# Ending the routed blocks two units sooner, and placing the first steps of the last layer beside the last two gated units

## The chip, the cores and the metric

The kernel runs on one core of a Trainium2 chip. The metric is the device time of one execution in microseconds; the time given for a kernel is the median of its runs. The core's engines work side by side, each through its own queue in order: TensorE (PE in the profile, its weight loads PEld), VectorE (DVE), ScalarE (ACT) and GpSimd (POOL); SyncE (SP) issues most DMAs, GpSimd issues the indirect ones. TensorE's results go to PSUM, eight banks, and are taken from there by VectorE or ScalarE.

## What is computed

Four layers, each of the form x = x + attention(norm(x)) + ffn(norm(x)), on 4 sequences of 512 tokens with 256 features in float32. What matters here is the end of layer 2 and the start of layer 3:

```
xn = layernorm(x)                                   # layer 2
x  = x + gated_attention(xn)                        # 16 heads, gated linear attention
       + latent_attention_and_experts(xn)           # 7 routed experts, top 2, and a shared one
xn = layernorm(x)                                   # layer 3
x  = x + xn + causal_attention(layernorm(xn)*g + b) # one head of 256 features
       + routed_moe(xn)                             # 8 experts of width 512, top 2, softmax of the two logits
```

## The kernel before

**Tiling.** x lies in on-chip memory as 16 tiles of 128 tokens, 4 to a sequence (b = 0 to 3). `xn` is its norm, `xnT` the transposed norm.

**Layer 2** (`layer2`, line 992) runs 32 gated units, one for each pair of heads and each sequence; unit u belongs to sequence u mod 4. A unit is split into three generators: `gated_supply` (line 1129: keys, queries, their exponentials, prepared one unit ahead), `gated_unit` (line 1174: scores, sums, softmax, products, gate, root of squares) and `gated_drain` (line 1314: transposes and output products of the unit before, which add into x). `run(u, beside, rate)` steps them in an order written as a string, line 1032: "m" is the unit, "s" the next one's supply, "d" the last one's drain. After each letter it takes `rate` steps, on average, of a further generator `beside`. For units 0 to 23 that is the latent attention; for units 24 to 30 it is `routed2` (line 1065): the dispatch of the tokens to 38 blocks of 128 slots, then for each block a fetch of weights and rows, a transposition, the hidden products and the output, which a GpSimd indirect DMA sends to a table in memory (`send_back`, line 330). Ahead of unit 31 the rest of `routed2` is run, and `collect` (line 338) reads the table back, two tiles of 256 KB for each two tiles of x, and adds them into x on VectorE. The order that the engines see is set by a scheduler from the order of the program and from its own model of durations; only in layer 3 is TensorE's order that of the program (line 1681).

**Layer 3** (`layer3`, line 1655) loads its weights, then for each sequence takes the norm (`layer_norm3`, line 1758: sums on VectorE, powers on GpSimd, and a second norm's scale `again`), the transposed features and the router (`route3`, line 1772: eight logits a token, the best two, softmax). Beside sequences 1 and 2 it starts the causal attention of sequences 0 and 1. `causal` (line 1789) is a generator whose first step adds xn into x on GpSimd, scales y on ScalarE, transposes it to yT and makes four qk products; the further steps are v, four steps of scores, the last transposition, the product with v, and the output. When all four routers are done, `dispatch` (line 158) counts the tokens of each expert (the rank and count matmuls), gives each a slot, and builds the table of slots with 64 small matmuls, eight `slots_on` steps; these are called beside the attention of sequences 0 and 1 from step 8 of their remaining steps on. Then 39 blocks run through the stages fetch, features, hidden, a pause and output, with the attention of sequences 2 and 3 beside them; `collect` and the stores of x end the kernel.

**Memory.** The latent attention's constants (rk, up, ow, rotk, rotq, va, and the tile mt of maxima) are tiles of a pool from layer 0 to the end of layer 2 (`latent_ahead`, line 1344). `Ring` is a helper that cuts tiles out of a given piece of memory by tag. In layer 2 four PSUM banks belong to the gated units (tag "ps") and, from unit 24 on, four to the routed blocks (tag "ex").

## Time and profile before

| | |
|---|---|
| median of 3 runs | 2320.91 us (2320.03 to 2325.61) |
| the profiled execution | 2334.37 us, of which the span from first to last instruction is 2332.6 us |
| mean granted TensorE clock | 0.909 |
| PE busy | 2019.1 us (87%) |
| DVE busy | 1240.0 us (53%) |
| ACT busy | 841.1 us (36%) |
| POOL busy | 625.8 us (27%) |
| the chain that ended last | PE 64%, DVE 12%, issue 10%, DMA 6%, POOL 5%, ACT 3% |

Times in the profile are microseconds from the start of the span. A line such as "L1216 PE MATMUL pt<-Wg,xnT 128x256 x8" is a run of eight matmuls issued at line 1216 that write tile pt from Wg and xnT; a float32 matmul of the program is two instructions. The granted clock is the share of TensorE's full speed that was allowed in the stretch. The profile cuts the span also into stages given by their ends, and then shows for each the busy time of every engine; busy time of TensorE times the clock is the work done, as it would be counted at full clock.

### The profile page before, as it was taken

To read this page: it belongs to the slowest core of one execution; us is meant where nothing else is said; L and a number is where in the kernel's file an instruction comes from. 1 tells how busy PE (TensorE), PEld (TensorE's weight loads), DVE (VectorE), ACT (ScalarE), POOL (GpSimd) and SP (SyncE) were. 2 spreads that over 40 slices of the span, in tenths; PEclk is the share of its full clock that TensorE was granted. 3 is DMA by queue.
4 is the path that set the end of the run, shared out by engine and by line. 5 is a ranking of instruction groups with operands and counts; after the bars stand their busy time and mean duration, and the time that the engine had idled before them with its cause. 6 is when DMAs were issued, how large, how long until landed. Compare 5 with 4: busy or idle time off the path is not lost.

```text
span 2332.6 us, 36307 instructions
## 1 busy us (share of the span) xinstructions
PE 2019.1 (87%) x13455; PEld 1501.4 (64%) x13455; DVE 1240.0 (53%) x3682; ACT 841.1 (36%) x1729; POOL 625.8 (27%) x737
## 2 busy tenths in 40 slices
PE   6754088874999999999999999999999968899995
PEld 2453077762566676666766676656778755678995
DVE  5765056657655655565565656546555564422223
ACT  1110056552334443343344444332354413344221
POOL 5334634443111121111111121110444332012331
PEclk8855599996999999999999999998999977899998
DMA  9911378874000000000000000001433220166897
GB/s 314 331 42 58 108 271 280 281 255 146 1 8 10 6 12 6 5 17 6 4 14 5 8 10 5 8 10 39 133 113 110 86 79 19 61 224 237 291 330 242
DMA packets 152536, 244.02 MB, mean 105 GB/s; under 512 B 15846, under 2 KB 111944, under 8 KB 152232
## 3 DMA queue, kind: packets, MB, share of 16 engines
q1 hardware_dynamic: 137336, 199.50, 26.3%
q0 software_dynamic: 15024, 42.20, 5.2%
q8 instruction: 107, 1.75, 0.3%
q14 instruction: 69, 0.57, 0.1%
HBM read 190.41 MB, written 66.58 MB: 110 GB/s over the span
## 4 chain that ended last, share of the span: by engine, by line
PE 64%; DVE 12%; issue 10%; DMA 6%; POOL 5%; ACT 3%; SPq 1%; another core or an unknown queue 0%; POOLq 0%; DVEq 0%; ACTq 0%
PE pt L1216 7%; PE pj L1138 6%; PE g L1742 5%; PE o L1329 4%; PE kq L1551 3%; PE sc L1201 3%; PE pov L1280 2%; PE gu L959 2%; PE o L1755 2%; DMA r<-l_rows,in_slot 2%; PE qk L1519 2%; DVE junk L1526 2%; PE pv L1567 2%; DMA r<-l_rows 2%; PE qkp L1804 1%
## 5 line engine op out<-in xcount | busy, mean ns | idle before, releaser
L334 POOL DMA_INDIRECT l_outs<-y,to x172 | 168.5, 980 | 325.5 <-ACT y L333 243.2
L306 DVE TENSOR_TENSOR mine<-r,number 128x2 f32<-128x2 f32 (+1 forms) x96 | 15.5, 161 | 273.9 <-DMA r<-l_rows,in_slot 207.2
L294 POOL DMA_INDIRECT r<-l_rows,in_slot x77 | 77.1, 1001 | 276.9 <-PE rt L325 147.0
L1742 PEld LDWEIGHTS g<-rT,we 128*128 128x128 f32 x1248 | 145.2, 192 | 5.2 <-ACT rT L327 3.4
L1742 PE MATMUL g<-rT,we 128*128 128x128 f32 x1248 | 145.9, 275 | 2.4 <-ACT rT L327 2.4
L1526 DVE CUSTOM_DVE_ANT_0 junk<-qk,hide 128x512 f32<-128x512 f32 (+3 forms) x256 | 124.7, 487 | 43.5 <-PE qk L1519 24.9
L1559 POOL TENSOR_SCALAR_AFFINE_SELECT pr<-pr 128x512 f32<-128x512 f32 x64 | 40.2, 639 | 339.3 <-ACT pr L1556 339.3
L959 PE MATMUL gu<-rT,we 128*128 128x128 f32 x760 | 112.5, 287 | 21.4 <-issue 9.7
L325 PE MATMUL rt<-ident,r 128*128 128x128 f32 x344 | 67.1, 295 | 70.2 <-DMA r<-l_rows 69.0
L327 ACT COPY rT<-rt 128x256 f32<-128x256 f32 x172 | 62.6, 372 | 178.3 <-PE rt L325 103.1
L1329 PE MATMUL o<-Wo,oT 128*128 128x256 f32 x512 | 126.2, 390 | 0.0
L959 PEld LDWEIGHTS gu<-rT,we 128*128 128x128 f32 x760 | 104.3, 198 | 33.7 <-issue 16.3
L1216 PE MATMUL pt<-Wg,xnT 128*128 128x256 f32 x512 | 124.2, 394 | 1.3 <-PE ot L1322 0.5
L333 ACT ACTIVATE y<-o,share 128x256 f32<-128x256 f32 x172 | 81.2, 473 | 114.9 <-PE o L1755 48.1
L1207 DVE TENSOR_TENSOR s<-sc,keep 128x512 f32<-128x512 f32 x128 | 82.5, 684 | 72.4 <-PE sc L1201 72.3
L1216 PE MATMUL pt<-Wv,xnT 128*128 128x256 f32 x512 | 120.1, 385 | 0.0
L1151 DVE RECIPROCAL rz<-rz 128x128 f32<-128x128 f32 x128 | 117.5, 935 | 0.4
L1216 PEld LDWEIGHTS pt<-Wg,xnT 128*128 128x128 f32 x512 | 97.0, 195 | 26.0 <-issue 7.1
L413 PE MATMUL tr<-ident,xn 128*128 128x128 f32 x160 | 33.7, 357 | 85.8 <-DVE xn L398 81.3
L1216 PEld LDWEIGHTS pt<-Wv,xnT 128*128 128x128 f32 x512 | 95.0, 191 | 15.1 <-DVE st L387 0.2
L1556 ACT ACTIVATE pr<-kq 128x512 f32<-128x512 f32 (+1 forms) x192 | 86.2, 530 | 50.1 <-PE kq L1551 49.5
L325 PEld LDWEIGHTS rt<-ident,r 128*128 128x128 f32 x344 | 53.9, 203 | 77.6 <-issue 75.0
(457 smaller groups left out, 4565.1 us busy)
## 6 DMA issues: line engine op xcount, KB each, us to landing
we<-l_packed SPq DMA_DIRECT2D x133, 384.0 KB
we<-l_w SPq DMA_DIRECT2D x78, 512.0 KB
we<-l_wo SPq DMA_DIRECT2D x39, 512.0 KB
l_rows<-none SPq DMA_DIRECT2D x1, 12920.0 KB
r<-l_rows SPq DMA_DIRECT2D x19, 680.0 KB
xn<-l_outs SPq DMA_DIRECT2D x32, 256.0 KB
l_rows<-xn SPq DMA_DIRECT2D x8, 544.0 KB
l_packed<-l_w_gate SPq DMA_DIRECT2D x1, 4096.0 KB
```

Of the source, the lines that this page charges most:

```text
L325: nc.tensor.transpose(pt[:, k, :], r[:, :D].rearrange("p (d k) -> p k d", k=KD)[:, k, :], self.ident)
L333: nc.scalar.activation(y, ps, AF.Copy, scale=share)
L334: self.no_order(moe["name"] + " back", nc.gpsimd.indirect_dma_start(out=moe["outs"][:, :], out_offset=bass.IndirectOffsetOnAxis(ap=to, axi ...
L959: nc.tensor.matmul(ps[:, q, :], we[:, q, k * P : (k + 1) * P], rT[:, k, :], start=(k == 0), stop=(k == KD - 1))
L1138: nc.tensor.matmul(ps, w[n][:, k, :], self.xnT[:, k, t["b"] * T : (t["b"] + 1) * T], start=(k == 0), stop=(k == KD - 1))
L1151: inverse = lambda c: nc.vector.reciprocal(rz[:, c * P : (c + 1) * P], rz[:, c * P : (c + 1) * P])
L1207: nc.vector.tensor_tensor(s, ps[hh], keep4, ALU.mult)
L1216: nc.tensor.matmul(ps[:, i, :], self.xnT[:, k, s : s + P], w[n][:, k, :], start=(k == 0), stop=(k == KD - 1))
L1329: nc.tensor.matmul(ps[:, p, :], of_parity(oT[:, h, c * D : (c + 1) * D], p), wo[:, h, :], start=(h == 0), stop=(h == 1),)
L1526: nc.vector.tensor_tensor_reduce(out=junk[:, :m], in0=tiles[j][:, off : off + m], in1=self.hide[:, T - m :], op0=ALU.add, op1=ALU.max, sca ...
L1556: nc.scalar.activation(pr[:, j, off : off + m], tiles[j][:, :m], AF.Exp, scale=0.25)
L1742: nc.tensor.matmul(pt[:, m, :], we[:, q, k * T + m * P : k * T + (m + 1) * P], rT[:, k, :], start=(k == 0), stop=(k == KD - 1),)
```

## The change

The routed blocks are stepped at 1.45 a letter instead of 1.25 and end with unit 29. `collect` takes a range of tiles, and for layer 2 it adds the two parts of a token on GpSimd first, so that VectorE adds once. It runs step by step beside unit 30, at 0.75 a letter, with the norm and router of sequence 0 (`ended2`). Beside unit 31, at 1.0 a letter, run norms and routers of sequences 1 and 2 (`ahead3`). The last unit's letters leave the supply out and have its drains sooner. Beside the last drain lie the first three steps of the causal attention of sequence 0. Layer 3's router state, loads and first tiles need memory at that time: they lie in two pieces, `both` and `mt`, that are shared with the latent attention's constants (`router3`); and their PSUM tiles come from the "ex" banks through an alias in `Ring`. `route3` and the first part of `causal` have more yields, and the add of xn into x comes after the qk products. Layer 3 then begins with the norm of sequence 3, v of sequence 0 and the products of sequence 1; the slots begin at step 4 of the remaining attention steps.

```diff
@@ -58,7 +58,11 @@
 
         self.base, self.free = base, 0
 
+    alias = None
+
     def tile(self, shape, dtype, tag, name, bufs=None):
+        if self.alias:
+            return self.pool.tile(shape, dtype, tag=self.alias, name=name)
         if tag not in self.places and self.pool is None:
             n = 1
             for d in shape[1:]:
@@ -89,6 +93,9 @@
         nc.gpsimd.memset(self.rows[:, :, D:], 0.0)
         self.xn = self.rows[:, :, :D]
         self.xnT = state.tile([P, KD, NB * T], F32, tag="xnT", name="xnT")
+
+        self.mt = state.tile([P, 4, P], F32, tag="mt", name="mt")
+        self.both = state.tile([P, 6144], F32, tag="both", name="both")
...
@@ -335,9 +342,9 @@
             out=moe["outs"][:, :], out_offset=bass.IndirectOffsetOnAxis(ap=to, axis=0), in_=y, in_offset=None
         ))
 
-    def collect(self, moe, wk):
-
-        for i in range(0, NTILE, 2):
+    def collect(self, moe, wk, of=range(0, NTILE, 2)):
+
+        for i in of:
             x = self.x[:, i : i + 2, :]
             ys = []
             for m in range(moe["k"]):
@@ -345,7 +352,7 @@
                 s = (m * NTILE + i) * P
                 self.load(y, moe["outs"][s : s + 2 * P, :].rearrange("(n p) d -> p n d", p=P))
                 ys.append(y)
-            if len(ys) > 2:
+            if len(ys) > 2 or moe is self.moe2:
                 self.nc.gpsimd.tensor_tensor(ys[0], ys[0], ys.pop(), ALU.add)
             for y in ys[1:] + ys[:1]:
                 self.nc.vector.tensor_tensor(x, x, y, ALU.add)
@@ -1029,7 +1036,7 @@
                 drain = self.gated_drain(units[u - 1]) if u else iter(())
                 credit = 0.0
                 chains = {"m": self.gated_unit(units[u]), "s": supply, "d": drain}
-                for what in "mmmmsmsmmdmmsmsdmsd":
+                for what in "mmmmsmsmmdmmsmsdmsd" if u + 1 < UNITS else "mmmmdmmdmmdmmm":
                     next(chains[what], None)
                     credit += rate
                     while credit >= 1:
@@ -1051,16 +1058,40 @@
                     pass
             wk = tp("ex", 4)
             gp["ex"] = tp("exps", 4, space=PSUM)
+            self.router3()
             routed = self.routed2(wk)
-            for u in range(first, UNITS):
-                if u == UNITS - 1:
-                    for _ in routed:
-                        pass
-                    self.collect(moe, wk)
-                run(u, routed, 1.25)
-            for _ in self.gated_drain(units[UNITS - 1]):
+            for u in range(first, UNITS - 2):
+                run(u, routed, 1.45)
+            for _ in routed:
                 pass
+            run(UNITS - 2, self.ended2(wk, gp["ex"]), 0.75)
+            run(UNITS - 1, self.ahead3(gp["ex"]), 1.0)
+            drain = self.gated_drain(units[UNITS - 1])
+            for chain in (self.units3[0], self.units3[0], drain, self.units3[0], drain, drain):
+                next(chain, None)
         self.held.close()
+
+    def ended2(self, wk, pool):
+
+        for i in range(0, NTILE, 2):
+            self.collect(self.moe2, wk, (i,))
+            yield
+            if i == 2:
+                self.layer_norm3(0)
+        yield from self.route3(0, pool, "ex")
+
+    def ahead3(self, pool):
+
+        self.layer_norm3(1)
+        for _ in range(3):
+            yield
+        yield from self.route3(1, pool, "ex")
+        for _ in range(5):
+            yield
+        self.layer_norm3(2)
+        for _ in range(2):
+            yield
+        yield from self.route3(2, pool, "ex")
 
     def routed2(self, wk):
 
@@ -1345,9 +1376,12 @@
 
         nc, a, NR = self.nc, self.a, 7
         tile = lambda n, *shape: wp.tile(list(shape), F32, tag=n, name=n)
-        kvq, rk, up = tile("kvq", P, KD, P), tile("rk", P, KD, T), tile("up", P, 2, T)
-        vu, ow, ln1, shift_row = tile("vu", 64, D), tile("ow", P, KD, D), tile("ln1", P, D), tile("shift_row", P, 1)
-        rotk, rotq = tile("rotk", P, T), tile("rotq", P, 2, T)
+        both = Ring(self.both, None)
+        cut = lambda n, k, m: both.tile([P, k, m], F32, tag=n, name=n, bufs=1)
+        kvq, rk, up = tile("kvq", P, KD, P), cut("rk", KD, T), cut("up", 2, T)
+        vu, ow, ln1, shift_row = tile("vu", 64, D), cut("ow", KD, D), tile("ln1", P, D), tile("shift_row", P, 1)
+        rotk, rotq = cut("rotk", 1, T)[:, 0, :], cut("rotq", 2, T)
+        va = cut("va", 4, 512).rearrange("p a (b c) -> p a b c", c=32)
         rw, rb, ln2, sh = tile("rw", P, KD, NR), tile("rb", 1, NR), tile("ln2", P, D), tile("sh", P, 3, D)
         kp = lambda ap: ap.rearrange("(k p) n -> p k n", p=P)
         self.load(kvq, kp(a["l2_kvq"]))
@@ -1370,7 +1404,7 @@
             self.load(sh[:, q].rearrange("p (k i) -> p k i", k=KD), kp(a["l2_sh_" + n]))
         self.load(sh[:, 2], a["l2_sh_down"])
         self.w2, self.top2 = tile("w2", P, NTILE, 8), tile("top2", P, NTILE, 8)
-        mt, va, sign = tile("mt", P, 4, P), tile("va", P, 4, 16, 32), tile("sign", P, 1)
+        mt, sign = self.mt, tile("sign", P, 1)
...
@@ -1654,50 +1688,39 @@
 
     def layer3(self):
         nc, a = self.nc, self.a
-        NE = 8
         with ExitStack() as ctx:
             tp = lambda n, bufs, **k: ctx.enter_context(self.tc.tile_pool(name=n, bufs=bufs, **k))
             self.wexp = tp("wexp3", 4)
             wp = tp("l3w", 1)
-            w = wp.tile([P, NTILE, NE], F32, tag="w", name="w")
-            top = wp.tile([P, NTILE, NE], F32, tag="top", name="top")
             moe = self.moe3
-            gw = wp.tile([P, KD, NE], F32, tag="gw", name="gw")
-            self.load(gw, a["l3_gate_w"].rearrange("(k p) n -> p k n", p=P))
-            wa, wk, we = tp("l3a", 1), tp("l3k", 2), tp("l3e", 4)
-            self.ps3 = ps3 = {n: tp("l3" + n, bufs, space=PSUM) for n, bufs in (("tr", 2), ("mm", 4), ("sm", 2))}
-            self.again = {}
-            ptr, psm = ps3["tr"], ps3["sm"]
...
+            self.wk3, we = tp("l3k", 2), tp("l3e", 4)
+            self.ps3 = ps3 = {n: tp("l3" + n, bufs, space=PSUM) for n, bufs in (("tr", 2), ("sm", 2), ("mm", 4))}
+            psm = ps3["sm"]
 
 
             with self.tc.manual_schedule(engines={mybir.EngineType.PE}):
-                units = [self.causal(b, gb, qkv, ow, wk, ps3) for b in range(NB)]
-                for b in range(NB):
+                units = self.units3
+                route = self.route3(NB - 1, psm, "sm")
+                with self.tc.high_priority():
+                    self.layer_norm3(NB - 1)
+                next(units[0])
+                for _ in range(2):
                     with self.tc.high_priority():
-                        self.layer_norm3(b)
-                        self.to_features(ptr, self.xn[:, 4 * b : 4 * b + 4, :], self.xnT[:, :, b * T : (b + 1) * T])
-                        self.route3(b, gw, wk, psm, w, top)
-                    if b in (1, 2):
-                        next(units[b - 1], None)
+                        next(route)
+                    next(units[1])
+                next(units[1])
                 pieces = self.wexp.tile([P, 3, 4, D], F32, tag="we", name="pieces")
                 pieces = Ring(pieces.rearrange("p q e d -> p (q e d)"), None)
-                slots = self.dispatch(moe, self.rows, top, w, pieces, psm, "sm", wp)
+                slots = self.dispatch(moe, self.rows, self.top3, self.w3, pieces, psm, "sm", wp)
 
                 def slots_on():
                     with self.tc.high_priority():
                         return next(slots, slots) is None
 
                 slots_on()
+                next(units[1])
                 for n, _ in enumerate(step for pair in zip(units[0], units[1]) for step in pair):
-                    if n >= 8:
+                    if n >= 4:
                         slots_on()
                 while slots_on():
                     pass
@@ -1755,6 +1778,30 @@
             self.nc.tensor.matmul(o, h[:, m, :], we[:, 2, m * D : (m + 1) * D], start=(m == 0), stop=(m == 3))
         self.send_back(self.moe3, o, to, share, wk)
 
+    def router3(self):
+
+        mt = self.mt.rearrange("p a b -> p (a b)")
+        cut = lambda at, a, b: mt[:, at : at + a * b].rearrange("p (a b) -> p a b", b=b)
+        self.w3, self.top3, self.gw3 = cut(0, NTILE, 8), cut(P, NTILE, 8), cut(2 * P, KD, 8)
+        self.cut3 = Ring(mt[:, 2 * P + 16 :], None, {"lg": (2, 4, 14), "ex": (2, 4, 8)})
+        self.gb3 = cut(2 * P + 16 + 112 + 64, 2, KD)
+        self.load(self.gw3, self.a["l3_gate_w"].rearrange("(k p) n -> p k n", p=P))
+        self.again = {}
+        both = Ring(self.both, None)
+        cut = lambda n, k, m: both.tile([P, k, m], F32, tag=n, name=n, bufs=1)
+        self.qkv3, self.ow3 = cut("qkv", KD, 3 * D), cut("ow", KD, D)
+        self.load(self.qkv3, self.a["l3_qkv"].rearrange("(k p) n -> p k n", p=P))
+        self.load(self.ow3, self.a["l3_o_proj"].rearrange("(k p) n -> p k n", p=P))
+        gb = self.gb3
+        for m in range(2):
+            for k in range(KD):
+                self.load(gb[:, m, k : k + 1], self.a["l3_gb"][m, k * P : (k + 1) * P].unsqueeze(1))
+        self.both3 = {n: cut(n, k, m) for n, k, m in (("y", 4, D), ("yT", KD, T), ("qk", 4, T))}
+        ex = Ring(None, self.gp["ex"])
+        self.ps3 = {n: ex for n in ("tr", "mm", "sm")}
+        ex.alias = "ex"
+        self.units3 = [self.causal(b) for b in range(NB)]
+
     def layer_norm3(self, b):
 
         nc = self.nc
@@ -1769,41 +1816,49 @@
         self.rsqrt(c, v, 1.0, 1e-5)
         self.again[b] = c
 
-    def route3(self, b, gw, wk, psm, w, marks):
-        nc = self.nc
-        ps = psm.tile([P, 4, 8], F32, tag="sm", name="lg")
+    def route3(self, b, pool, tag):
+
+        nc, gw, wk = self.nc, self.gw3, self.cut3
+        self.to_features(pool, self.xn[:, 4 * b : 4 * b + 4, :], self.xnT[:, :, b * T : (b + 1) * T], tag)
+        yield
+        ps = pool.tile([P, 4, 8], F32, tag=tag, name="lg")
         for i in range(4):
             for k in range(KD):
                 nc.tensor.matmul(ps[:, i, :], self.tokens(k, 4 * b + i), gw[:, k, :], start=(k == 0), stop=(k == KD - 1))
-        lg = wk.tile([P, 4, 14], F32, tag="lg", name="lg")
+        lg = wk.tile([P, 4, 14], F32, tag="lg", name="lg", bufs=2)
         nc.gpsimd.memset(lg, NEG)
         nc.vector.tensor_copy(lg[:, :, :8], ps)
         top, v8 = self.top_weights(lg, 8, 2)
-        nc.vector.tensor_copy(marks[:, 4 * b : 4 * b + 4, :], top)
-        ex = wk.tile([P, 4, 8], F32, tag="ex", name="ex")
+        nc.vector.tensor_copy(self.top3[:, 4 * b : 4 * b + 4, :], top)
+        ex = wk.tile([P, 4, 8], F32, tag="ex", name="ex", bufs=2)
         nc.vector.tensor_tensor(ex, lg[:, :, :8], v8[:, :, 0:1].to_broadcast([P, 4, 8]), ALU.subtract)
         nc.scalar.activation(ex, ex, AF.Exp)
         nc.vector.tensor_tensor(ex, ex, top, ALU.mult)
-        self.share(w[:, 4 * b : 4 * b + 4, :], ex)
-
-    def causal(self, b, gb, qkv, ow, wk, ps3):
-
-        nc = self.nc
-        ptr, pmm = ps3["tr"], ps3["mm"]
+        self.share(self.w3[:, 4 * b : 4 * b + 4, :], ex)
+        yield
+
+    def causal(self, b):
+
+
+        nc, qkv, ow = self.nc, self.qkv3, self.ow3
         x, xn = (t[:, 4 * b : 4 * b + 4, :] for t in (self.x, self.xn))
-        nc.gpsimd.tensor_tensor(x, x, xn, ALU.add)
-        y = wk.tile([P, 4, D], F32, tag="y", name="y")
+        place = lambda n, k, m: self.wk3.tile([P, k, m], F32, tag=n, name=n, bufs=1) if b % 2 else self.both3[n]
+        y = place("y", 4, D)
         for i in range(4):
             nc.scalar.activation(y[:, i, :], xn[:, i, :], AF.Copy, scale=self.again[b][:, i : i + 1])
-        yT = wk.tile([P, KD, T], F32, tag="yT", name="yT")
-        self.to_features(ptr, y, yT, gb=gb)
-        qk = wk.tile([P, 4, T], F32, tag="qk", name="qk")
+        yT = place("yT", KD, T)
+        self.to_features(self.ps3["tr"], y, yT, gb=self.gb3)
+        yield
+        qk = place("qk", 4, T)
         for m in range(4):
-            ps = pmm.tile([P, T], F32, tag="mm", name="qkp")
+            ps = self.ps3["mm"].tile([P, T], F32, tag="mm", name="qkp")
             for k in range(KD):
                 nc.tensor.matmul(ps, qkv[:, k, m * P : (m + 1) * P], yT[:, k, :], start=(k == 0), stop=(k == KD - 1))
             nc.scalar.copy(qk[:, m, :], ps)
-        yield
+            if m % 2:
+                yield
+        ptr, pmm, wk = self.ps3["tr"], self.ps3["mm"], self.wk3
+        nc.gpsimd.tensor_tensor(x, x, xn, ALU.add)
         v = wk.tile([P, 4, D], F32, tag="v", name="v")
         for j in range(0, 4, 2):
             ps = pmm.tile([P, 2, D], F32, tag="mm", name="vp")
```

## The prediction

> **What bounds the kernel now.** I read four views: the page's busy slices, the engines by stage, the timelines of TensorE, VectorE and GpSimd round the change of layers, and the groups of instructions in single windows. By stage (start:end, length, then busy microseconds and instruction counts of PE, PEld, DVE, ACT, POOL, then granted clock, DMA share, GB/s):
>
> ```profile
> 1836.00:1875.50 39.50, 37.01 (x266) 29.30 (x262) 19.87 (x53) 16.47 (x35) 13.50 (x15) 1.00 0.20 62
> 1875.50:1933.20 57.70, 34.05 (x201) 27.21 (x200) 34.30 (x76) 8.98 (x15) 26.41 (x32) 0.76 0.24 75
> 1933.20:1975.90 42.70, 34.98 (x145) 23.54 (x145) 16.68 (x101) 18.99 (x45) 6.23 (x15) 0.79 0.09 26
> 1975.90:2055.10 79.20, 70.43 (x266) 48.59 (x266) 33.61 (x176) 25.97 (x65) 3.42 (x4) 0.85 0.32 112
> 2055.10:2306.80 251.70, 249.95 (x1784) 232.50 (x1784) 66.09 (x303) 82.80 (x168) 71.87 (x74) 1.00 0.77 260
> ```
>
> The stages are gated unit 30; unit 31 with its drain; norms, features and routers of layer 3; dispatch and attention of sequences 0 and 1; expert blocks. Units and blocks are TensorE at full clock. The three stages between are not: busy time times clock is 25.9, 27.6 and 59.9, so 113.4 us of full-clock work takes 179.6 us, and 66.2 us are lost. The timelines show how (start, length, instruction, in brackets the idle time before it and what ended it; PE, then DVE, then POOL):
>
> ```profile
> 1909.89 1.12 PE L1269 MATMUL pvt<-ident,pv 128*128 128x128 f32 x4 [13.98 <-ACT pv L1256]
> 1913.80 3.61 PE L1329 MATMUL o<-Wo,oT 128*128 128x256 f32 x8
> 1919.99 2.00 PE L1329 MATMUL o<-Wo,oT 128*128 128x256 f32 x8
> 1926.42 0.66 PE L1322 MATMUL ot<-ident,o 128*128 128x128 f32 x4 [4.43 <-POOL o L1309]
> ...
> 1898.56 2.08 DVE L351 TENSOR_TENSOR x<-x,sum 128x512 f32<-128x512 f32 x1
> 1900.66 0.65 DVE L351 TENSOR_TENSOR x<-x,sum 128x512 f32<-128x512 f32 x1
> 1906.35 2.23 DVE L351 TENSOR_TENSOR x<-x,sum 128x512 f32<-128x512 f32 x1
> ...
> 1897.21 2.89 POOL L1794 TENSOR_TENSOR x<-x,xn 128x1024 f32<-128x1024 f32 x1
> ```
>
> Unit 31 waits 14 us because its softmax step stands on VectorE behind the collect's sixteen adds and three norms; then the same eight matmuls take 3.61 us instead of 2.00.
>
> **Part 1: routed blocks in six units.** Seven windows from 1597.5 (unit 24) to 1875.5 sum to 259.1 us of busy times clock in 278.0: 18.9 lost, 14.2 of it in the first two, where dispatch holds VectorE. A block costs 1.7 us (gu 0.95, rt 0.25, o 0.5, start to start in the PE timeline), 38 blocks 64.6, the dispatch matmuls about 8; the rest over seven is 26.6 us for a unit with the next one's supply. 161 routed steps need 19 x 1.45 = 27.5 a unit, 165 in six. TensorE work is the same, denser: 259.1 - 26.6 + about 17.9 lost = 250.4, so unit 30 starts at 1848 instead of 1836. Below: two microseconds less loss. Above: a gather takes about 3.5 us from issue to its reader (POOL 1804.16, DVE 1807.63), and the distance between fetch and use falls from 3/1.25 = 2.4 to 3/1.45 = 2.1 unit steps of 2.0 us, 4.8 to 4.2 us. That still holds it; I add nothing.
>
> Layer 3's seven loads move to unit 24: 3.2 us of SP's queue by their rows at 1933. SP's next work there, the row stores and fetches, waits for dispatch (the first gather is at 1631), and the matrices' space is free once latent attention has made its last keys. Nothing; at worst 3 us.
>
> **Part 2: unit 30 with collect, norm and router of sequence 0.** TensorE: 26.6 + 2.9 (eight transposes and sixteen router matmuls, the 1956.4 to 1959.8 rows at clock 0.79) = 29.5. VectorE: own unit 10.5, supply 5.6 (four reciprocals of 0.94, scan 1.22, clamp 0.69), eight adds at 0.67 = 5.4, norm 3.1, router and copies 3.4: 28.0. The other eight adds go to GpSimd: o<-o,rs, 128x512, is 2.03 for two, so about 1.0 each, 8 in all. Here a rule speaks against the change: the Trainium skill (GPSIMD Engine Reference, Key points) says that GpSimd shares its SBUF interfaces with VectorE and collides with instructions that have two SBUF inputs. The trace agrees: an add took 2.08 and 2.23 with a GpSimd add beside it, 0.65 without. By the rule taken fully, all 8 us come back on VectorE: 36. By the row, where 1.4 us were lost in a GpSimd add of 2.9, half: 32. The collect also waits once for its sums (3.3 us in the trace). I take **34**, between 30 and 38; unit 31 starts at 1882 instead of 1875.5.
>
> **Part 3: unit 31 without collect.** TensorE: 26.6 less supply 6.0 = 20.6 (unit 30's drain is in it), plus 2.9 for sequence 1: 23.5. VectorE: 10.5 + two norms, two routers = 23.5. Its chain, sc to pov, is some 17 us by the durations of the rows and 0.25 us a hand-over. I take 27 (24 to 33): pov ends at 1909. From pov to the first ot is 7.4 us (1920.0 to 1927.4: squares, products, sums, power and scaling on GpSimd). Beside it now lie sequence 2's features and router 2.9 and y with two qk products 4.4. Then ot 1.0, two qk products 3.5, o 4.3, add 0.8: x is final at 1926 (was 1934.2).
>
> **Part 4: to the dispatch.** Norm of sequence 3: 4.3 us (1934.2 to 1938.5), with v of sequence 0 (about 4) beside it. If the moved x+xn add gets in front of its power on GpSimd, 2.4 more. Transposes 1.0, copies 0.9, router 2.0: 1934. The marks (2.0 on VectorE) are ready at 1936; in front of the rank matmul in TensorE's order stand four qk products of sequence 1, 7 to 8 us: rank at **1942**, was 1975.9.
>
> **Part 5: to the first expert.** The 79.2 us from rank to the first g lose v of sequence 0 (half of 9.4) and the qk products of sequences 2 and 3 with their waits (2033.9 to 2054.0 less 2.2 for transposes that stay, 17.9): 56.6, g at 1998.6. Those products are not gone: a causal unit has two more steps, and they come back in rounds of the blocks at full clock, 32 x 0.43 = 13.8. What they covered is late next: the gather, and the first expert's weights, 1.5 MB issued at 2035.7; at the window's 350 to 390 GB/s that is some 7 us with the latency. But the slots start one pair of steps sooner and end before the last attention products, whose 8.8 us and 2 of transposes now cover it. Nothing; at worst 5 us.
>
> **The sum.** 1998.6 + 251.7 + 13.8 + 25.8 (2306.8 to the end) = 2289.9 against a span of 2332.6: **42.7 less**. The profiled execution took 2334.4, the median of the runs is 2320.9; I take the same microseconds off: **2278**.
>
> **Clock, row against rule.** The skill (TensorE: Matmul & The Clock Gate, Part 1) lets the clock fall to half after an idle window of about 3.4 us. The rows are stricter: after a gap of 2.40 us at 1643.8, two o matmuls take 1.22 instead of 0.70; gaps of 0.98 and 1.23 cost nothing. By the rule units 30 and 31, with gaps of one engine's work, run full: their 53 us of work in 55 or so. By the row each gap over 2 us adds up to 4. My 61 for both holds two of them.
>
> **Rivals.**
> - Half the gain. Without blocks to fill them the two units wait on VectorE and on their own chain at reduced clock, like units 24 and 25, which took 43 and 45 us: +9 and +18 on mine, **2305**. For it: 28 to 36 us of VectorE in unit 30. Against: no sixteen adds in front of a softmax.
> - More gain. The gaps fill as in units 26 to 29 (98% busy): 30 and 24 for the two, 5 less at the rank, 3 of clock after it: 15 more, **2263**. For it: TensorE has ready work almost everywhere. Against: three hand-overs at the end have none.
> - Nothing moves. The early products are held by the shared space or PSUM buffers until the old place; then only collect is hidden: perhaps 10, **2311**. Against: space and banks are free by unit 30.
> - Slower. In units 25 to 29 TensorE waits for each denser gather. Above 42.7 / 38 = 1.12 us a block the change loses; at 1.5 us, 57 in all, **2335**. For it: VectorE already waits for gathers, 9.3 us in the window 1762 to 1798, and GpSimd's queue holds gathers, send-backs and the units' scaling in one order. Against: TensorE waited there for no gather, and 4.2 us still exceed 3.5.
>
> **Chances.** Forecast 0.55 (own range 2264 to 2294), half 0.22, more 0.10, nothing moves 0.05, slower 0.08. The range **2258 to 2308** leaves out the slower case, most of the unmoved one and the far ends. Within 0.3% (7 us, about what a measurement tells from no change) falls a piece of the last two: faster 0.87, same 0.04, slower 0.09.
>
> **What would show it.** Right: no idle before pvt above 2 us in unit 31; collect's adds between unit 30's start and 18 us later; qk products of sequence 0 between pov and ot; rank near 1942; first g near 1999; g to last o about 266. Wrong: TensorE waits on gathers between 1640 and 1850 above 10 us in all; unit 30 or 31 above 40 us with a clock under 0.9; g idle for weights above 5 us; a block stage above 275, which would give the start back.

## The result, and the profile after

Six runs of the changed kernel gave a median of 2302.18 us (2297.2 to 2309.9), beside 2319.69 us for the kernel before (six runs, 2312.02 to 2325.61): a ratio of 0.9929, 95% interval 0.9901 to 0.9957. The change gains 17.5 us, 0.41 of the 42.7 that were forecast. The direction is right and the time lies inside the stated range, but most of the gain did not come.

The two profiled executions cannot be subtracted as they are. Their spans differ by 37.2 us (2332.6 and 2295.4), but layer 2's dispatch already starts at 1602.7 in the one and 1582.9 in the other, 19.7 us apart, after code that the change hardly touches (the last experiment looks at this). From the rank matmul of that dispatch on, the kernel before takes 729.9 us and the changed one 712.5: 17.4 us. All stages below are counted from there. That these 17.4 us meet the medians so closely is partly luck: this profile is of the fastest of the six runs, and a second one of the changed kernel (c_after below) takes 722.0. First the engines by stage in the changed kernel (columns as in the prediction): dispatch to unit 25, unit 25, units 26 to 29, unit 30, unit 31 to the end of pov, pov to layer 3's rank matmul, rank to the first g, the blocks.

```profile
1582.90:1623.90 41.00, 38.24 (x201) 33.15 (x199) 33.00 (x147) 8.69 (x16) 4.05 (x5) 0.71 0.32 107
1623.90:1678.70 54.80, 48.89 (x317) 40.11 (x316) 27.26 (x102) 23.56 (x50) 23.53 (x24) 0.91 0.41 125
1678.70:1836.40 157.70, 153.79 (x1111) 124.91 (x1110) 91.66 (x279) 76.50 (x157) 67.50 (x69) 1.00 0.36 108
1836.40:1880.20 43.80, 35.27 (x223) 27.32 (x222) 28.28 (x70) 15.65 (x29) 21.84 (x21) 0.84 0.32 100
1880.20:1913.20 33.00, 27.78 (x215) 23.77 (x214) 18.35 (x63) 8.67 (x17) 14.70 (x21) 0.95 0.00 1
1913.20:1945.30 32.10, 30.03 (x125) 19.43 (x124) 13.87 (x63) 18.24 (x37) 9.62 (x15) 0.95 0.00 1
1945.30:2003.80 58.50, 48.08 (x219) 35.75 (x217) 30.42 (x167) 21.67 (x58) 3.33 (x4) 0.88 0.27 94
2003.80:2269.90 266.10, 263.89 (x1816) 238.49 (x1816) 66.55 (x306) 87.52 (x176) 71.91 (x74) 1.00 0.77 258
```

The same view of the kernel before, for the first six of these stages (the last two stand in the prediction):

```profile
1602.70:1640.90 38.20, 35.38 (x199) 29.42 (x198) 33.13 (x149) 8.69 (x16) 4.04 (x5) 0.82 0.34 110
1640.90:1686.90 46.00, 42.66 (x293) 34.84 (x292) 25.68 (x90) 19.00 (x42) 20.16 (x20) 0.96 0.41 126
1686.90:1835.40 148.50, 146.41 (x1061) 118.75 (x1060) 85.47 (x265) 69.47 (x143) 62.21 (x62) 1.00 0.34 107
1835.40:1875.50 40.10, 37.61 (x271) 29.89 (x270) 20.47 (x54) 16.84 (x36) 13.50 (x15) 1.00 0.20 61
1875.50:1920.00 44.50, 25.67 (x170) 20.61 (x169) 27.60 (x60) 6.53 (x11) 17.22 (x20) 0.73 0.31 98
1920.00:1975.90 55.90, 43.36 (x179) 30.13 (x177) 23.39 (x116) 21.45 (x49) 15.42 (x27) 0.81 0.07 20
```

As in the prediction, the length of a stage less busy time times clock is what TensorE loses there. The figure is good to about 2 us a stage: from dispatch to unit 25 the two kernels run the same matmuls, and busy time times clock is 29.0 in the one and 27.2 in the other. In microseconds, worked out from such rows of both kernels:

| stage | length before | after | forecast | lost before | lost after |
|---|---|---|---|---|---|
| dispatch to unit 30 | 232.8 | 253.4 | 245.4 | 16.3 | 28.0 |
| unit 30 | 40.1 | 43.8 | 34 | 2.5 | 14.2 |
| unit 31 to the end of pov | 44.6 | 33.1 | 27 | 25.8 | 6.6 |
| pov to rank | 55.8 | 32.1 | 33 | 20.8 | 3.6 |
| rank to the first g | 79.2 | 58.5 | 56.6 | 19.3 | 16.2 |
| blocks | 251.6 | 266.1 | 265.5 | 1.7 | 2.2 |
| tail | 25.9 | 25.5 | 25.9 | | |

TensorE's work is the same to within 2 us. The change is a trade in lost time: the end of layer 2 and the start of layer 3 lose 39.5 us less, and 23.9 of these are given back in units 24 to 30 and the blocks. The rest, 15.6 us, is nearly the whole gain. Where it is given back shows in the timelines of the changed kernel (GpSimd, VectorE and TensorE, in order of time):

```profile
1631.65 1.00 POOL L301 DMA_INDIRECT r<-l_rows,in_slot  x1 [0.30 <-issue]
1636.56 0.16 DVE L313 TENSOR_TENSOR mine<-r,number 128x2 f32<-128x2 f32 x1 [4.20 <-DMA r<-l_rows,in_slot]
1638.82 1.22 PE L1138 MATMUL o<-we,h 128*128 128x256 f32 x2 [3.61 <-DVE h L1133]
...
1839.80 1.04 POOL L341 DMA_INDIRECT l_outs<-y,to  x1 [0.17 <-issue]
1847.11 1.25 POOL L356 TENSOR_TENSOR sum<-sum 128x512 f32<-128x512 f32 x1 [6.27 <-DMA sum<-l_outs]
1848.39 0.69 DVE L358 TENSOR_TENSOR x<-x,sum 128x512 f32<-128x512 f32 x1 [5.95 <-POOL sum L356]
1853.09 1.12 PE L1280 MATMUL okt<-ident,ok 128*128 128x128 f32 x4 [5.77 <-DVE ok L1276]
1861.96 5.77 PE L1247 MATMUL pt<-Wg,xnT 128*128 128x256 f32 x16
...
1888.54 1.04 PE L1353 MATMUL ot<-ident,o 128*128 128x128 f32 x8
...
1902.93 0.60 PE L1300 MATMUL pvt<-ident,pv 128*128 128x128 f32 x4
```

The last line is the one that waited 13.98 us before: in unit 31 pvt waits for nothing now, as forecast. But a wait of the same kind stands in unit 30. The last send-back is issued at 1839.80, the first sum can be added only at 1847.11, and VectorE, whose queue has that first add ahead of `ok`, stands still for 5.95 us. TensorE waits 5.77 us for ok, and then sixteen Wg matmuls take 5.77 us instead of 3.72 at the lower clock. In all, VectorE waits 10.0 us for sums in this unit (by groups, idle time at the end):

```profile
L358 DVE TENSOR_TENSOR x<-x,sum 128x512 f32<-128x512 f32 x8 | 7.0, 871 | 10.0 <-POOL sum L356 10.0
```

In unit 25 a gather comes late, VectorE waits for it 4.20 us and TensorE 3.61 for what VectorE then does.

### The profile page after: what moved, and what is told of

Read it like the earlier page. It is cut to its first block, busy times and chain, and to the rows that moved or that the text cites. A ratio compares the mean times of both kernels' runs of the same rounds, so it can differ in the third digit from the quotient of the medians.

```text
span 2295.4 us, 36311 instructions
## 1 busy us (share of the span) xinstructions
PE 2000.7 (87%) x13455; PEld 1491.9 (65%) x13455; DVE 1232.8 (54%) x3669; ACT 849.5 (37%) x1740; POOL 638.1 (28%) x745
## 4 chain that ended last, share of the span: by engine, by line
PE 61%; DVE 9%; issue 8%; DMA 5%; POOL 4%; ACT 3%; SPq 0%; POOLq 0%; DVEq 0%; ACTq 0%
PE pt L1247 7%; PE pj L1169 6%; PE g L1765 5%; PE o L1360 4%; PE kq L1585 3%; PE gu L966 3%; PE pov L1311 3%; PE sc L1232 3%; PE o L1778 2%; DMA r<-l_rows,in_slot 2%; PE qk L1553 2%; DVE junk L1560 2%; DMA r<-l_rows 2%; PE pv L1601 2%; PE o L979 1%
## 5 line engine op out<-in xcount | busy, mean ns | idle before, releaser
L1593 POOL TENSOR_SCALAR_AFFINE_SELECT pr<-pr 128x512 f32<-128x512 f32 x64 | 40.2, 639 | 338.5 <-ACT pr L1590 338.5
L420 PE MATMUL tr<-ident,xn 128*128 128x128 f32 x160 | 35.2, 360 | 87.6 <-DVE xn L405 80.4
L1247 PEld LDWEIGHTS pt<-Wv,xnT 128*128 128x128 f32 x512 | 96.4, 194 | 15.6 <-DVE st L394 0.2
```

The costliest lines, as they stand in the source:

```text
L1247: nc.tensor.matmul(ps[:, i, :], self.xnT[:, k, s : s + P], w[n][:, k, :], start=(k == 0), stop=(k == KD - 1))
```

## The experiments

Lengths in microseconds from one profile of each kernel, same stages; the ratio is to the kernel before on the same chip. The two profiles of the changed kernel differ by 9.5 us from dispatch to the end, so a difference of a few microseconds in that column says nothing by itself.

| run | to unit 30 | unit 30 | unit 31 | pov to rank | rank to g | dispatch to end | ratio (95% interval) |
|---|---|---|---|---|---|---|---|
| before | 232.8 | 40.1 | 44.6 | 55.8 | 79.2 | 729.9 | |
| c_before | 232.7 | 39.9 | 45.0 | 57.3 | 77.7 | 730.9 | |
| changed | 253.4 | 43.8 | 33.1 | 32.1 | 58.5 | 712.5 | 0.9929 (0.9901 to 0.9957) |
| c_after | 254.3 | 44.5 | 40.2 | 31.6 | 60.1 | 722.0 | 0.9942 (0.9925 to 0.9958) |
| e1_behind | 252.0 | 45.1 | 35.0 | 31.6 | 60.1 | 714.2 | 0.9948 (0.9928 to 0.9968) |
| e2_vector | 256.6 | 46.2 | 36.1 | 35.0 | 60.2 | 726.2 | 0.9927 (0.9910 to 0.9944) |
| e3_thin | 252.3 | 42.9 | 32.0 | 33.3 | 60.4 | 714.0 | 0.9932 (0.9911 to 0.9952) |
| e4_both | 249.7 | 44.7 | 36.3 | 32.1 | 60.2 | 712.7 | 0.9939 (0.9920 to 0.9959) |
| f1_nocollect | 253.7 | 32.8 | 33.3 | 31.1 | 59.4 | 702.1 | |
| g2_vecbehind | 254.7 | 39.1 | 31.9 | 31.5 | 59.9 | 709.4 | 0.9922 (0.9904 to 0.9941) |
| f2_later | 251.1 | 39.2 | 33.3 | 32.1 | 58.4 | 705.1 | 0.9912 (0.9890 to 0.9935) |
| f5_behind_q | 252.1 | 34.0 | 33.6 | 33.2 | 60.5 | 705.0 | 0.9897 (0.9880 to 0.9913) |
| g1_lead | 252.7 | 43.4 | 36.0 | 35.0 | 60.2 | 717.9 | 0.9930 (0.9913 to 0.9946) |
| f3_seven | 232.5 | 40.1 | 48.0 | 36.5 | 60.3 | 710.5 | 0.9918 (0.9901 to 0.9935) |
| f4_seven_q | 235.2 | 40.3 | 27.6 | 49.5 | 60.8 | 704.9 | 0.9874 (0.9858 to 0.9891) |
| f6_seven_ms | 235.0 | 41.3 | 27.4 | 43.8 | 59.4 | 699.1 | 0.9860 (0.9839 to 0.9881) |

### Unit 30: what of the collect costs

**Queue or load.** Two edits, each alone. The first puts collect's VectorE adds behind unit 30's softmax step (and steps the collect at 1.0 a letter instead of 0.75, to make up for the later start); the second takes the eight adds off GpSimd.

```diff
 def ended2(self, wk, pool):                      # e1_behind
+    yield from (None for _ in range(7))
     for i in range(0, NTILE, 2):
-        self.collect(self.moe2, wk, (i,))
+        with self.tc.issue_after(self.pv.ins): self.collect(self.moe2, wk, (i,))
...
-            if len(ys) > 2 or moe is self.moe2:  # e2_vector
+            if len(ys) > 2:
```

> VectorE's adds of the collect are queued behind the softmax step of unit 30 (its subtraction pv), the loads stay where they are. Theory, the queue: in the changed kernel VectorE stands 5.95 us at the first add, waiting for the last block's way through memory, while the softmax step behind it is ready, and TensorE's clock falls after it. Then unit 30, from its first sc to that of unit 31, falls from 43.8 us to 36 (33 to 39), its clock from 0.84 to over 0.93, no wait of TensorE in it over 2.5 us, and the whole is 6 to 9 us faster than the changed kernel: ratio to the kernel before about 0.990. Rival, the load: VectorE's 28 us and GpSimd's adds on shared interfaces hold unit 30; then it stays at 41 or more and the ratio at 0.993.

> Both parts of a token are added on VectorE again, sixteen adds in unit 30, none on GpSimd. Rival, the load: if the adds on GpSimd cost VectorE more than they save, unit 30 falls from 43.8 to below 41. Theory, the queue: VectorE waits at the first add for the same memory, about 5 us, so unit 30 stays between 42 and 48, longer by up to the 4 us of the eight added adds; ratio 0.993 to 0.995.

Unit 30 takes 45.1 and 46.2 us. The second result is what the queue theory expected, the first is where the load theory put it, so neither theory is enough alone. In the first run the wait for ok is gone, and two others, of 4.4 and 3.7 us, have come (waits of TensorE in unit 30: microseconds in all, times, longest):

```profile
PE tr L420 <- DVE xn L1812: 4.4, 1, 4.4
PE pj L1169 <- DVE ev L1224: 3.7, 1, 3.7
```

Its timelines of GpSimd and VectorE show why ev and the norm are late:

```profile
1851.20 6.78 POOL L356 TENSOR_TENSOR sum<-sum 128x512 f32<-128x512 f32 x4 [1.55 <-DMA sum<-l_outs]
1852.97 1.74 DVE L358 TENSOR_TENSOR x<-x,sum 128x512 f32<-128x512 f32 x1 [1.16 <-POOL sum L356]
1854.63 2.29 DVE L1181 TENSOR_TENSOR_SCAN rz<-one_col,eF 128x512 f32<-128x512 f32 x1
...
1863.92 1.26 POOL L356 TENSOR_TENSOR sum<-sum 128x512 f32<-128x512 f32 x1 [1.11 <-DMA sum<-l_outs]
1865.27 0.19 POOL L384 TENSOR_SCALAR rs<-mv 128x4 f32<-128x4 f32 x1
1866.76 1.38 DVE L1812 TENSOR_SCALAR xn<-x,mv,rs 128x256 f32<-128x256 f32 x4 [5.23 <-POOL rs L385]
```

ev is late by collisions: four GpSimd adds take 1.7 us each instead of 1.26, and beside them a VectorE add takes 1.74 instead of 0.65 and the scan 2.29 instead of 1.22. The norm is late by GpSimd's queue: its power `rs` stands behind GpSimd's own adds, each of which waits for its load, and VectorE waits 5.23 us for it. Four more runs take the collect apart.

**No collect at all.** The kernel leaves the collect out, so layer 3 gets x without the routed experts; it was run once.

```diff
     for i in range(0, NTILE, 2):
-        self.collect(self.moe2, wk, (i,))
         yield
```

> The changed kernel without the collect: the loads of the gathered sums and their sixteen adds are left out, norm, router and everything else stay. Unit 30 took 43.8 us with it. If the collect (its waits and its load on VectorE and GpSimd) is what makes unit 30 long, the unit takes 35 us or less at a clock above 0.95, and its TensorE loses under 5 us. The rival, that a unit without blocks beside it waits on its own chain of scores, softmax and products and drops the clock whatever stands on VectorE, expects 40 us or more.

The windows view of its unit 30:

```profile
1834.20:1866.90 32.70, 30.22 (x221) 23.32 (x220) 19.60 (x58) 15.58 (x29) 9.76 (x13) 1.00 0.02 5
```

32.7 us at full clock, 2.5 lost. So unit 30 without blocks beside it does not fall into its own chain, and the collect costs it eleven microseconds. The rival that the prediction called "half the gain" (2305 us, against 2302 measured) was half right: unit 30 did wait on VectorE at reduced clock, but not on its own chain. That its total came so close is luck: it gave units 30 and 31 27 us more than the forecast, and of the 25.1 us by which the stages missed, 9.8 and 6.1 lie in these two and 8.0 ahead of them.

**Both edits, and where the adds stand.** g2 makes both edits. f2 also puts sequence 0's transposes and router matmuls behind the second scores (`issue_after` on their last matmul). f5, on top of f2, moves twelve of the sixteen adds from behind the softmax step to behind the masks of the second scores, so that they no longer stand in front of q; it also puts sequence 1's transposes behind unit 31's products.

```diff
-            with self.tc.issue_after(self.pv.ins): self.collect(self.moe2, wk, (i,))
+            with self.tc.issue_after((self.pv if i < 4 else self.sv).ins): self.collect(self.moe2, wk, (i,))
```

> Collect behind unit 30's softmax step and all its adds on VectorE, but sequence 0's transposes left where the scheduler puts them: one of the two edits that took unit 30 from 45.1 us (adds on GpSimd too, behind the softmax) to 39.2 us. If it is GpSimd's adds that stretch VectorE's queue, unit 30 takes 39 to 41 us; if it is the place of the transposes in TensorE's order, 43 to 46.

> Collect's adds behind unit 30's softmax step, all on VectorE (none on GpSimd), and sequence 0's transposes and router matmuls behind the unit's second scores in TensorE's order. The first collect experiment took away the 5.8 us wait for ok and got waits of 3.7 us (ev) and 4.4 us (the norm) in its place. If these are what is left, unit 30 falls from 45 to 36 to 40 us and the ratio to the kernel before to 0.990. The rival, that the sum of collect, norm and the unit's own steps on VectorE sets the length wherever they stand, expects 43 us or more and 0.993 or above.

> As the run with the late collect (ratio 0.9912), but in unit 30 twelve of the sixteen adds stand behind the masks of the second scores and no longer in front of q, for which TensorE waited 6.7 us; sequence 1's transposes and router matmuls stand behind unit 31's products pok. If waits of TensorE on VectorE's queue are what is left, unit 30 falls from 39.2 to 33 to 35 us (32.8 without any collect), unit 31 from 33.3 to 30 to 32, layer 2's dispatch to the end to 697 to 701 us, ratio 0.987 to 0.989. The rival, that the collect is only pushed in front of the norm of sequence 1, expects unit 31 at 36 us or more, 703 us or more and 0.991 again.

Unit 30 falls from 45.1 to 39.1 us with GpSimd's adds gone (g2: the wait behind ev is gone, the one for the norm is 3.8 us); the place of the transposes adds nothing (f2, 39.2); with the adds behind q as well it takes 34.0 us, its windows row:

```profile
1849.50:1883.50 34.00, 31.10 (x221) 23.54 (x220) 24.87 (x49) 14.09 (x27) 9.64 (x12) 1.00 0.41 128
```

Fifteen of the sixteen adds lie in this unit, all on VectorE, and it is 1.3 us longer than without any. What cost the ten microseconds was the order in VectorE's queue and GpSimd's adds beside it, not the amount of VectorE work (28.3 us busy in the changed kernel, 24.9 here). Unit 31 did not get the 30 to 32 us expected of f5 (33.6), and from dispatch to the end f5 is no better than f2: the 5.2 us come back in small pieces, 1.0 to unit 30, 1.1 from pov to rank, 2.1 from rank to g. The two executions of the changed kernel differ by as much in such stages (1.6 from rank to g), so whether these pieces belong to the edit stays open; the ratio, over four runs on another chip, did fall, from 0.9912 to 0.9897, with intervals that overlap.

### Units 24 to 29: what the denser blocks cost

**Thinner where dispatch runs.** e3 keeps the old rate in units 24 and 25 and takes 1.55 in the four behind; e4 adds the edit of e1.

```diff
             for u in range(first, UNITS - 2):
-                run(u, routed, 1.45)
+                run(u, routed, 1.25 if u < first + 2 else 1.55)
```

> The routed blocks are stepped at 1.25 a letter, as before, in units 24 and 25, and at 1.55 in units 26 to 29. Theory, the filling: the first blocks are stepped faster than GpSimd's queue, which holds the gathers, the send-backs and the unit's scaling, can fetch them, and VectorE stands at the first reader of a gather. Then rank to unit 26 falls from 95.8 us to 84 to 89, units 26 to 29 rise from 157.7 by about 3 to 5 (some 8 steps, two blocks, move there), and the whole is 4 to 8 us faster: ratio about 0.990. Rival, the density: the same wait comes in each dense unit; then what is won in the first two is lost in the four, the sum of both stays at 253 and the ratio at 0.993.

> The edits of the runs with the adds behind the softmax step and with thin first units, together. If both theories hold they add: about 13 us faster than the changed kernel, ratio 0.987 (0.985 to 0.990). If only one holds, its own ratio; if neither, 0.993.

The last two windows rows of e3 on this stretch, unit 25 and units 26 to 29:

```profile
1628.30:1674.50 46.20, 42.72 (x295) 34.90 (x294) 25.69 (x90) 19.03 (x42) 20.13 (x20) 0.96 0.40 126
1674.50:1842.40 167.90, 158.49 (x1135) 129.35 (x1134) 90.22 (x291) 76.09 (x161) 71.44 (x73) 0.99 0.35 109
```

Unit 25 has its old length (46.2 instead of 54.8), but units 26 to 29 now lose 11.0 us instead of 3.9 (167.9 less 158.49 x 0.99), and the sum moves by 1 us. The loss is not tied to dispatch; it comes with the density, wherever that is put. With the adds behind the softmax step as well (e4) the ratio is 0.9939: neither theory held, alone or together.

**Blocks fetched one sooner.** An empty stage stands between fetch and features, and there are four buffers of rows instead of three.

```diff
-        stages = self.fetch2, self.features2, self.hidden2, self.output2
+        stages = self.fetch2, lambda t, wk, *state: state, self.features2, self.hidden2, self.output2
...
-                    yield
+                    if s != 1: yield
```

> The changed kernel with each block's weights and rows fetched one block sooner (an empty stage between fetch and features, four buffers of rows instead of three, the same 1.45 steps). In the changed kernel's unit 25 VectorE waited 4.2 us for a gather and TensorE 3.6 us behind it, the clock fell, and the unit took 54.8 us (44.5 of TensorE work). If the distance between gather and use is what is too short, unit 25 takes 47 to 50 us, units 26 to 29 156 to 158, dispatch to unit 30 244 to 248 instead of 253. The rival, that the gathers still stand in GpSimd's queue behind the units' scaling and the send-backs, or that dispatch holds VectorE, expects unit 25 at 52 us or more and 251 to 255.

Between the two: unit 25 takes 51.0 us, units 26 to 29 160.7, and the whole 252.7, as before. In unit 25 the gather is late again, from GpSimd's timeline and VectorE's:

```profile
1647.89 1.04 POOL L1340 TENSOR_TENSOR o<-o,rs 128x512 f32<-128x512 f32 x1
...
1651.41 0.99 POOL L301 DMA_INDIRECT r<-l_rows,in_slot  x1 [0.16 <-issue]
1654.62 0.16 DVE L313 TENSOR_TENSOR mine<-r,number 128x2 f32<-128x2 f32 x1 [4.83 <-DMA r<-l_rows,in_slot]
```

The gather is issued at 1651.41 because the unit's scaling and a send-back stand ahead of it on GpSimd, and 3.2 us later it is used. A fetch that the program makes sooner leaves it behind the same work. That the distance in the program is too short is therefore not the answer; how much of the 8 us is GpSimd's queue and how much VectorE's was not separated.

The kernel before shows it already. The reader of the pair that gave the 3.5 us (POOL 1804.16, DVE 1807.63) had stood waiting for it, and so VectorE does at most gathers, in both kernels alike (waits of VectorE and TensorE in units 25 to 29, kernel before and then changed: microseconds in all, times, longest):

```profile
1807.63 0.16 DVE L306 TENSOR_TENSOR mine<-r,number 128x2 f32<-128x2 f32 x1 [2.44 <-DMA r<-l_rows,in_slot]
...
DVE mine L306 <- DMA r<-l_rows,in_slot: 51.0, 23, 5.9
PE o L1107 <- DVE h L1102: 4.6, 4, 2.4
...
DVE mine L313 <- DMA r<-l_rows,in_slot: 50.8, 27, 5.3
PE o L1138 <- DVE h L1133: 7.5, 6, 3.6
```

The denser blocks did not make VectorE wait longer for its gathers, but TensorE waits longer behind them. The likely reason is that less other work lies between two blocks; no run tests it.

**Seven units of blocks.** The blocks go back to the seven units and the rate of the kernel before; collect (behind the softmax step), norms and routers of sequences 0 to 2 lie in unit 31 and its drain, and all adds are VectorE's. The rest of the change stays.

```diff
-            for u in range(first, UNITS - 2):
-                run(u, routed, 1.45)
+            for u in range(first, UNITS - 1):
+                run(u, routed, 1.25)
...
-            run(UNITS - 2, self.ended2(wk, gp["ex"]), 0.75)
-            run(UNITS - 1, self.ahead3(gp["ex"]), 1.0)
+            tail = self.ended2(wk, gp["ex"])
+            run(UNITS - 1, tail, 2.0)
```

> The blocks end one unit sooner instead of two (seven units at the old rate of 1.25), and collect, norms and routers of sequences 0 to 2 lie in unit 31 and its drain, collect behind the unit's softmax step and on VectorE alone. If the losses of the first units come from the denser blocks alone, dispatch to unit 30 takes 233 us again, unit 30 40 us, 20 us less than in the changed kernel; unit 31 with collect then takes 36 to 42, pov to the rank matmul 40 to 48, and the ratio is 0.988 to 0.991. The rival, that what is won there is lost again behind unit 31, where VectorE has collect and three norms in a row, expects 0.993 or above.

> As the run with seven units of blocks, but in unit 31 only the first four adds of collect and sequence 0's norm stand behind the softmax step; the other twelve stand on VectorE behind the masks of the second scores. In the run before, TensorE waited 13.4 us for q behind fourteen of these adds (two of them 2.5 us long beside GpSimd's 5.3 us add). If that queue is what made unit 31 48 us long, it takes 34 to 38 us, pov to the rank matmul 36 to 42, dispatch of layer 2 to the end 700 to 704 us and the ratio is 0.986 to 0.989. The rival, that the adds and norms are VectorE work that has to be done by the rank matmul wherever it stands, expects what unit 31 loses to come back before the rank matmul: 708 to 711, 0.991 or above.

Dispatch to unit 30 is 232.5 us again and unit 30 40.1: the old rate has the old loss. But unit 31 takes 48.0. TensorE, GpSimd and VectorE in it:

```profile
1888.11 2.08 PE L1234 MATMUL sc<-q,eF 64*128 64x128 f32 x16 [13.35 <-DVE q L1306]
1876.83 5.29 POOL L1863 TENSOR_TENSOR x<-x,xn 128x1024 f32<-128x1024 f32 x1
1876.23 3.69 DVE L358 TENSOR_TENSOR x<-x,sum 128x512 f32<-128x512 f32 x6
1880.05 2.63 DVE L358 TENSOR_TENSOR x<-x,sum 128x512 f32<-128x512 f32 x1
```

This is the wait of the kernel before in another place: q stands behind all sixteen adds, and one GpSimd add (5.29 us; 2.35 elsewhere in this unit) and the VectorE add beside it (2.63 instead of 0.65) hold each other up. With twelve adds behind the masks of the second scores and the routers spread over the drain (f4) unit 31 takes 27.6 us and the wait for q 2.58; 13 of the 20 us won come back between pov and rank (49.5), where sequence 1's norm stands behind the twelve adds and TensorE waits 5.23 us for it.

**The version that beats the changed kernel.** f6, on top of f4, puts the last eight adds, those of sequences 2 and 3, behind unit 31's sums of squares (`self.ms`); on the same chip the changed kernel ran again.

```diff
+        some((0, 2), self.pv)      # behind the softmax step
+        self.layer_norm3(0)
...
+        some((4, 6), self.sv)      # behind the masks of the second scores
+        self.layer_norm3(1)
...
+        some((8, 10), self.ms)     # behind the sums of squares
+        self.layer_norm3(2)
...
+        some((12, 14), self.ms)
```

> As the best run so far (seven units of blocks, ratio 0.9874), but the adds of collect for sequences 2 and 3 stand behind unit 31's sums of squares, so that sequence 1's norm, for which TensorE waited 5.2 us behind pov, comes after four adds instead of twelve. If VectorE's order is what is left there, pov to the rank matmul falls from 49.5 to 43 to 46 us and dispatch of layer 2 to the end from 705 to 699 to 702, ratio 0.985 to 0.987. The rival, that the eight adds come back in front of the norms of sequences 2 and 3 and delay the rank matmul as much, expects 48 us or more and 0.987 to 0.989.

> The changed kernel again, beside the one above and on the same chip. If the stages repeat as they did in the second profile of the kernel before, dispatch to unit 30 takes 253 us within 2, unit 30 44, unit 31 33, dispatch to the end 712 within 3, and the ratio lies between 0.990 and 0.996. A gain of the kernel above that is only the scatter between chips would leave both ratios within 0.003 of each other; a true one leaves 0.005 or more.

Unit 31 and pov to rank in f6's windows:

```profile
1877.00:1904.40 27.40, 23.77 (x186) 19.98 (x185) 16.67 (x39) 10.79 (x20) 9.61 (x12) 0.94 0.42 133
1904.40:1948.20 43.80, 39.69 (x176) 27.23 (x177) 32.06 (x136) 21.78 (x48) 22.05 (x33) 0.88 0.05 17
```

f6 takes 2299.4 us (2293.62 to 2305.37, five runs), the changed kernel beside it 2318.12 (2316.22 to 2323.77), the kernel before 2332.64: 0.9860 and 0.9942, with intervals that do not touch. By the windows it loses 57.6 us where the changed kernel lost 70.8 and, in its second execution, 80.4. Pov to rank, dispatch to the end and the ratio lie where they were expected. Two things differ from the changed kernel, though, the rate of the blocks and the place of the adds. The rate alone is not enough (f3, 0.9918), and against f5, which has the denser blocks and its adds in better places (0.9897), the gain is smaller, measured on another chip, and the intervals just meet. So it is shown that this version beats the changed kernel; that it does so by the old rate is shown only in the stages (235.0 us to unit 30 instead of 253).

The changed kernel's own second execution missed what was expected of it: 40.2 us in unit 31 and 722.0 from dispatch to the end. The last section shows what its clock did.

### What the difference ahead of the change is

> The kernel before again, for a second profile of it. If the 19.7 us by which its dispatch came later in the first profile (1602.7 against 1582.9) is the scatter of one execution, dispatch starts between 1580 and 1592 as in the five profiles of changed kernels, and the stages from there on have their lengths within 1 us: 233 to unit 30, 40, 45, 56, 79, 252. If the change also moved the layers ahead of it, dispatch starts at about 1600 again.

Dispatch starts at 1588.3, and the stages repeat within 0.5 us, but for the two around layer 3's rank matmul (1.5 each, in opposite directions). But "the scatter of one execution" is not the best reading of the 19.7 us. On two chips the kernel before took 2318 us, and in the eight profiles from there dispatch starts between 1580 and 1591; on three others it took 2332, and in the six profiles from there dispatch starts between 1594 and 1603, whatever the kernel. So the difference lies ahead of layer 2's dispatch and goes with the chip, or with the hour, as the three were all used later. That the first profile of before (2334.37 us) came from a chip of the second kind, and the runs shown with it (2320.91) from one of the first, fits this but was not recorded.

## Why the prediction was right in direction and wrong in size

- **Part 1, "I add nothing"** for the denser gathers: failed. Forecast 12.6 us later to unit 30, measured 20.6. Work grew by 9.1 us, as one seventh of the 64.6 us of blocks should; the loss, which I had left as it was, went from 16.3 to 28.0. The comparison of 4.2 us of distance with 3.5 from issue to reader took the gather as issued when the program asks for it. It waits on GpSimd behind the unit's scaling and the send-backs, its reader was already waiting in the kernel before, and fetching sooner did not help. 2.8 us of the miss lie ahead of unit 25, where the same matmuls took 38.2 us at clock 0.82 or 41.0 at 0.71: 41.0 in all nine profiles at 1.45, 38.2 in five of seven at 1.25. The lower clock can come at either rate and is likelier at the denser one. The rival "slower" had the mechanism; its size (57 us) was far off. The sign set for it, over 10 us of TensorE waiting on gathers, did not come (7.5): TensorE is idle for 12.4 of the 28.0 us, and the rest is clock.
- **Part 2, unit 30 = 34 us**: failed, the largest miss (43.8, at clock 0.84, one of the prediction's own signs of being wrong). The work was not too small: TensorE had 29.5 forecast and 29.6 measured (35.27 x 0.84), VectorE 28.0 and up to 4 us of collisions forecast and 28.28 measured with them. But a sum of busy times is a length only if the queue's order lets them overlap. "The collect also waits once for its sums" (3.3 us) was costed on VectorE alone; VectorE waited 10.0 us for sums, 5.95 of it at the first, and what stands behind the waiting add (ok, then eF, the scan and ev) was not followed. GpSimd's eight adds took 11.4 us, not 8. f1 and f5 show that the 34 was to be had with the adds behind q.
- **The rule against the change.** The Trainium skill (GPSIMD Engine Reference, Key points) says that GpSimd and VectorE collide on the memory interfaces they share. By the rule taken fully all eight microseconds would come back on VectorE, by the row half of them. The row's size holds: in unit 30 the eight adds took 7.0 us instead of 5.2, the scan 2.3 instead of 1.2 and the norm's scaling 2.3 instead of 1.4, 3.8 us in all. But with the adds behind the softmax step, taking GpSimd's off made the unit 6.0 us shorter (45.1 to 39.1), as the waits for the sums went too; and with the adds in front of it the same edit gained nothing (43.8, 46.2), as the order was the longer wait. Neither way of pricing the collision sees these two.
- **Part 3, unit 31 = 27 us**: failed by 6, and by 13 in the second execution. The cause given was right, and the 14 us wait is gone. Work was 26.4 instead of 23.5 (27.78 x 0.95), since sequence 2's transposes, its first router products and three transposes of y moved in front of pov, and TensorE waits four times between 0.88 and 1.71 us for the norms and the unit's own steps, 5.2 in all. This is read from the trace; no run tests it. One reading of the prediction is off here: from the end of pov to the first ot the kernel before took 6.4 us (1920.0 to 1926.4), not 7.4.
- **The clock.** That gaps of 0.98 and 1.23 us "cost nothing" holds for the two gaps that were looked at. The same trace has another: after 0.97 us at 1613.68 the granted clock was 0.73 from 1614 to 1620. So short gaps were costed at nothing on a selection.
- **Parts 4 and 5** held: pov to rank 32.1 (33), rank to g 58.5 (56.6), blocks 14.5 longer (13.8), g not idle for weights. Together they gained 30 of the 31.6 us forecast.
- **The base.** The stages' errors (8.0, 9.8, 6.1, -0.9, 1.9 and 0.6, less 0.4 in the tail) sum to 25.1 us, the miss to within rounding (42.7 less 17.4). In these two profiles nothing has to be explained outside these stages; the 37.2 us between the two spans, nearer to the forecast, are no support for it.

## What to carry to other kernels

When work is moved beside other work, go through the in-order queue of the engine that takes it: what will stand behind each instruction that can wait (for a DMA above all), and who waits for that; a sum of busy times against the stage's length is only the lower bound. Give the moved work its place explicitly, behind the last step of the chain it could hold up, and cut it into pieces so that only what is needed first goes first. When a pipeline is compressed, the loss of the denser stretch belongs in the sum, and two profiles are subtracted only from the last instruction that they have in common.

## What the hardware showed that was not expected

**A collision of VectorE with GpSimd is a wait for the end of the other's instruction.** In the fifteen profiles with a collect, 24 of its VectorE adds between unit 30 and layer 3's rank matmul took over 0.8 us instead of 0.65. Each of them ends 0.55 us after the end of a GpSimd instruction that had begun before it: in f3's rows GpSimd's add ends at 1882.12 and VectorE's at 1882.68, in the prediction's rows 1900.10 and 1900.64. In the other direction, GpSimd's add in f3 began while six VectorE adds ran, to 1879.92, and took 2.94 us longer than its like. So the price of one collision is not a share of the work; it is what is left of the other instruction when the second one comes. This is read from the traces; no run tests it.

**The same gaps do not always cost the same clock.** Unit 31 in the second execution of the changed kernel:

```profile
1898.90:1939.20 40.30, 35.17 (x215) 30.10 (x214) 18.50 (x63) 8.77 (x18) 14.69 (x21) 0.75 0.00 1
```

and two of its matmuls:

```profile
1905.94 1.52 PE L420 MATMUL tr<-ident,xn 128*128 128x128 f32 x8 [1.71 <-DVE xn L1812]
1907.29 1.79 PE L1353 MATMUL ot<-ident,o 128*128 128x128 f32 x8
```

The idle time is the same as in the first execution (5.1 and 5.2 us), and so is the gap of 1.71 us. In the first, ot took 1.04 us right behind it and the unit ran at 0.95; here it took 1.79, the clock stayed low for most of the next 15 us, and the unit took 40.3 us instead of 33.0. The rule that the prediction weighed (the Trainium skill, TensorE: Matmul & The Clock Gate, Part 1: half clock after an idle window of about 3.4 us) and the row it preferred (gaps over 2 us cost up to 4) both give one price for one gap; here a gap below both cost 7 us in one execution and nothing in the other. The page also calls the window free-running and its effect variable from run to run, which fits. A stage with short gaps has a range of lengths, not one, and a difference of some 5 us in one profile of such a stage tells nothing by itself.
